# Pre-norm attention with an FP8 feed-forward on one core: the fourth key block's norm and the weight's quantisation placed ahead of the first scores

## The chip, the core and the metric

The kernel runs on one core of one Trainium2 chip. The metric is device time in microseconds for one launch. A core has TensorE (PE, with weight loads PEld beside it), VectorE (DVE), ScalarE (ACT), GpSimd (POOL) and SyncE (SP, which here only issues DMAs). Each engine works through its own instructions in order and waits on semaphores.

## The reference

```python
def reference(x, wq, bq, wk, bk, wv, bv, wo, bo, weight):   # x: (2, 2048, 512) fp32
    # attention: 16 query heads, 2 key/value heads, head size 32
    h = layernorm(x)
    q, k, v = h @ wq + bq, h @ wk + bk, h @ wv + bv
    q, k = rope(q) * 32 ** -0.5, rope(k)
    attn = softmax(q @ k.T * 32 ** -0.5)     # per head; 8 query heads share one k and v
    x = x + (attn @ v) @ wo + bo
    # feed-forward in fp8 e4m3 with one scale for the tensor
    h = layernorm(x)
    w8, w_scale = quant_e4m3(weight)         # scale = max|weight| / 448; weight: (512, 512) bf16
    h8, h_scale = quant_e4m3(h)              # scale over all 4096 rows
    return x + bf16((h8 @ w8.T) * (h_scale * w_scale))
```

The quantised weight `w8` and its scale are used by the feed-forward alone, that is, after the last row of attention is done, since `h_scale` is a maximum over all rows.

## The kernel before, in words

The 4096 rows are eight blocks of 512 (`NBLK`), four for each of two sequences. The work has three parts.

**The front** (`L697` to `L728`). The keys and values of the first sequence's four blocks are made one after another by the generator `project_kv`: `layernorm_stats` (DVE, with one power on POOL for `rstd`), `normalized` (DVE makes the tile `xn_kv`, PE transposes it, ACT copies it into `xnT`), the projection `pk` (four steps on PE, ACT adds the bias), the rotation (`r_k` on PE, `u_k` on DVE), the transposes of the values (`tv`), `rope` on POOL, and `stack_keys`: each of two arrays (`kS`, and `dkS`, the differences to a key further back) is split into a rounded and a remaining half (ACT, POOL), stored to DRAM and loaded back in four pieces, all by SP's queue. The queries of the first block come from `project_q`; `stack_queries` splits, stores and reloads them as `qst`.

The generators yield where another piece may stand between. `together` takes steps from several of them in turn, `first(steps, n)` limits one to n steps, and `run` exhausts one. The order so written is the order of the instructions on each engine. `FRONT` is 13 steps: the statistics, the normalised tiles and all transposes of a block. `MIDDLE` is 5 steps: the projection and the rotation's matmul. `PART` is 8 scores.

The front also makes the first unit's score maxima (`scores_for_maxima`): 32 score matmuls (L517) of 128 queries by 512 keys, each followed by a maximum on DVE (L524), sorted so that each eight of them need one more key block. They are taken eight at a time between the pieces of the fourth key block. The last eight need the fourth block's `kS`. Then the 8 maxima of each row are gathered, transposed and copied by ACT to `mT` (L546), and the rounds can begin.

**The rounds.** A unit is 256 queries of one quad (four heads); there are 8 units to a block and 64 in all. A unit has four rounds of four key chunks. In each round PE makes the scores again (L967) against the maxima, ACT takes the exponential (L976), POOL and an accumulating DMA add up the probabilities, and PE multiplies with the values (L913). Between these, the score maxima of the next unit are made (L517, L524), and `fill` takes pieces from a queue of jobs: the projections of later keys and queries, the output projection of finished blocks (L301, `po`) with the residual added on DVE, and the second norm. A job's step has a kind (for PE, for DVE or other) and is taken at a fixed place of the round.

`ask` puts the jobs of a block into the queue in the block's first unit, in round 2. Their inputs share a pool of three buffers (`x`), and `take_x` waits until the one three before is done. The residual's `x` of the block before is asked for only when at most two jobs are in the queue. In the last block but one, `ask` also loads the feed-forward's weight into one of these buffers and queues `prepare_weight`:

```python
            if n == NBLK - 2:
                take_x("w")
                w_all = xpool.tile([P, DC, D], BF16, tag="x", name="w_ffn")
                nc.sync.dma_start(w_all, w_ffn.rearrange("(c p) k -> p c k", p=P))
                queue.append(Job(ending(prepare_weight(w_all), "w"), due=step[0] + 2))
```

`prepare_weight` (L645 to L671) takes a maximum of each of the weight's four chunks of 128 rows on DVE (L651) and of these (L655), carries it across the partitions through two small PE instructions (L217, L223) and back to DVE for scale and inverse, and then for each chunk: scale (L663), the exponent's bits (L234), the rounding constant (L237), add (L239) and subtract (L240) on DVE, four bf16 transposes on PE (L669) and a copy by ACT into `wT` (L670). Two working tiles a chunk come from `w2`, a pool of six buffers shared with the halves of keys and queries.

**The end.** The scale over all rows is formed, and each block is quantised, transposed, multiplied with `wT` and written.

Buffers that matter here: `p` (four buffers) holds `xn_kv` in the front and the probabilities in the rounds; `ps_t` has the two PSUM banks E and O, used in the front by all transposes and in the rounds by the scores.

Of the kernel before, what the change touches and what calls it, by code (L numbers as in the profile page):

```python
# [10 lines left out]
BF16 = mybir.dt.bfloat16  # L11
# [5 lines left out]
P = 128  # L17
# [10 lines left out]
def preln_attn_fp8_ffn_kernel(  # L28
# [37 lines left out]
    nc = tc.nc  # L66
    B, S, D = x.shape
# [3 lines left out]
    DC = D // P  # L71
    NBLK = B * NB
# [15 lines left out]
    xpool = ctx.enter_context(tc.tile_pool(name="x", bufs=3))  # L88
    keys = ctx.enter_context(tc.tile_pool(name="keys", bufs=1))
    wide = ctx.enter_context(tc.tile_pool(name="wide", bufs=1))  # L90
    ppool = ctx.enter_context(tc.tile_pool(name="p", bufs=4))
# [66 lines left out]
    def load_tables(n):  # L158
        blk = n % NB
        if attending[0] or n == 0:  # L160
            csb = cs.tile([P, 2, TB], F32, tag="cs", name=f"cs_{n}")
        else:
            csb = papool.tile([P, 2, TB], F32, tag="pa", name=f"cs_{n}")
        nc.sync.dma_start(csb[:, 0, :], cos_t[:, blk * TB : (blk + 1) * TB])
        nc.sync.dma_start(csb[:, 1, :], sin_t[:, blk * TB : (blk + 1) * TB])
        return csb
# [207 lines left out]
    def project_kv(n, xt, xnT, csb):  # L374
        b, blk = divmod(n, NB)
        yield from layernorm_stats(xt, mean1[:, n, :], rstd1[:, n, :], f"1_{n}")
        yield from normalized(n, xt, xnT, f"kv_{n}")
        if n > 0:
            nc.sync.dma_start(xnT_far[n], xnT)
        if b not in vX:  # L380
            vX[b] = wide.tile([P, NTS, GROUPS, HD], F32, tag="vX", name=f"vX_{b}", bufs=2)
        pk = bank(f"pk_{n}")
        yield from product(pk, lambda c: wkv_sb[:, c, :], lambda c: xnT[:, c, :])
        if blk == 0:
            nc.gpsimd.memset(kx[:, :BACK], 0.0)
        else:
            nc.gpsimd.tensor_copy(kx[:, :BACK], kx[:, TB:])
        kv = t2(f"kv_{n}")
        nc.scalar.activation(kv, pk, AF.Identity, bias=bkv_sb)
        give_back()  # L390
        if attending[0]:
            u = swapped(kv, KD, f"k_{n}")
        else:
            u = yield from rotated(kv, csb, f"k_{n}")
        yield ON_PE
        tv = bank(f"tv_{n}")
        for i in range(NT):
            nc.tensor.transpose(tv[:, i * P : (i + 1) * P], kv[:, i * P : (i + 1) * P], ident)
        nc.scalar.copy(
            vX[b][:, blk * NT : (blk + 1) * NT, :, :].rearrange("p i g d -> p i (g d)"),  # L400
            tv.rearrange("p (i k) -> p i k", i=NT)[:, :, KD:],
        )
        give_back()
        if attending[0]:
            beside.insert(0, Job(stack_keys(n, kv, u, csb), due=step[0] + 2))
        else:
            yield from stack_keys(n, kv, u, csb)
# [238 lines left out]
    def prepare_weight(w_all):  # L646
        w = [w_all[:, o, :] for o in range(DC)]
        wmax = small.tile([P, DC], F32, tag="wmax", name="wmax")
        for o in range(DC):
            yield ON_DVE  # L650
            nc.vector.tensor_reduce(  # L651
                wmax[:, o : o + 1], w[o], AX.X, ALU.max, apply_absolute_value=True
            )
        wmax1 = small.tile([P, 1], F32, tag="wmax1", name="wmax1")
        nc.vector.tensor_reduce(wmax1, wmax, AX.X, ALU.max)  # L655
        yield LATER
        yield ON_PE
        inv = const.tile([P, 1], F32, tag="winv", name="winv")
        quantized_scale(wmax1, w_scale, inv, "w")
        for o in range(DC):  # L660
            yield ON_DVE
            v = t2(f"w_scaled_{o}")
            nc.vector.tensor_scalar(v, w[o], inv, None, ALU.mult)  # L663
            magic = t2(f"w_magic_{o}")
            yield from round_e4m3(w[o], v, magic)
            yield ON_PE
            tp = bank(f"wtp_{o}", BF16)[:, :D].rearrange("p (c t) -> p c t", c=DC)
            for c in range(DC):
                nc.tensor.transpose(tp[:, c, :], w[o][:, c * P : (c + 1) * P], ident_bf)  # L669
            nc.scalar.copy(wT[:, :, o * P : (o + 1) * P], tp)  # L670
            give_back()  # L671


    def run(steps):
        for _ in steps:
            pass
# [4 lines left out]
    def together(*runs):  # L681

        live = list(runs)
        while live:
            for steps, n in list(live):
                for _ in range(n):
                    if next(steps, "end") == "end":
                        live.remove((steps, n))
                        break

    def first(steps, n):

        for _ in range(n):
            if next(steps, "end") == "end":
                return
            yield

    FRONT = 1 + 3 * NT
# [4 lines left out]
    with tc.manual_schedule():  # L703
        xnT = {
            0: wide_block("xnT", "xnT_kv_0"),
            1: wide_block("attn", "xnT_kv_1", 2),
            2: wide_block("attn", "xnT_kv_2", 2),
            3: wide_block("qst", "xnT_kv_3", 2),
        }
        kv = {n: project_kv(n, x_kv[n], xnT[n], tables[n]) for n in (0, 1)}  # L710
        q0 = project_q(0, xnT[0], tables[0])
        run(first(kv[0], FRONT))
        together((kv[0], 1), (first(kv[1], FRONT), 2))
        x_kv[3] = load_x(3, "kv")
        kv[2] = project_kv(2, x_kv[2], xnT[2], load_tables(2))
        queries = first(q0, 1 + QUERIES)
        together((kv[1], 1), (queries, 1), (first(kv[2], FRONT), 2))
        assert (0, 0) in q_raw
        stack_queries(0)
        nc.sync.dma_start(wo_sb, wo.rearrange("(c p) n -> p c n", p=P))  # L720
        queries = first(q0, QUERIES)
        together((kv[2], 1), (queries, 1))
        kv[3] = project_kv(3, x_kv[3], xnT[3], load_tables(3))
        together((first(kv[3], FRONT), 2), (first(scores, PART), 1))
        together((first(kv[3], MIDDLE), 1), (first(scores, PART), 1))
        together((kv[3], 1), (first(scores, PART), 1))
        run(first(scores, PART))
        gather_maxima(0, ps_s.tile([P, TB], F32, tag=s_bank(), name="mtp_0"))  # L728

# [24 lines left out]
    step = [0]  # L754
# [43 lines left out]
    def take_x(name):  # L798

        while len(x_taken) >= 3 and x_taken[-3] not in x_done:  # L800
            advance()
        x_taken.append(name)

    def ending(steps, name):
        yield from steps
        x_done.add(name)
# [30 lines left out]
    def ask(u):  # L837

        k, half = units[u]

        for m in unbiased:
            add_bias(x_res[m])
            biased.add(m)
            if m in without_x:
                without_x.pop(m).due = step[0] + 2
        unbiased.clear()
        n, quad = quads[k]
        if half == 0 and quad == 0:
            if NB + n < NBLK:
                m = NB + n  # L850
                take_x(f"kv_{m}")
                make = lambda m=m: wide_block("xnT", f"xnT_kv_{m}")
                steps = later(project_kv, m, load_x(m, "kv"), make)
                queue.append(Job(ending(steps, f"kv_{m}"), due=step[0] + 2, tables=True))
            if n + 1 < NBLK:
                take_x(f"q_{n + 1}")
                steps = later(project_q, n + 1, load_xnT(n + 1))
                queue.append(Job(ending(steps, f"q_{n + 1}"), due=step[0] + 2, tables=True))
            if n == NBLK - 2:
                take_x("w")  # L860
                w_all = xpool.tile([P, DC, D], BF16, tag="x", name="w_ffn")
                nc.sync.dma_start(w_all, w_ffn.rearrange("(c p) k -> p c k", p=P))
                queue.append(Job(ending(prepare_weight(w_all), "w"), due=step[0] + 2))

        soon = len(queue) <= 2 and u % (QUADS * HALVES) > 0 or n == NBLK - 1
        free = len(x_taken) < 3 or x_taken[-3] in x_done
        if n > 0 and n - 1 not in x_asked and soon and (free or len(queue) <= 1):
            x_asked.add(n - 1)
            take_x(f"res_{n - 1}")
            x_res[n - 1] = load_x(n - 1, "res")  # L870
            unbiased.append(n - 1)
            if n == NBLK - 1:
                take_x(f"res_{n}")
                x_res[n] = load_x(n, "res")
                unbiased.append(n)
        if n == NBLK - 1 and quad == 3 and half == 0:

            fetch_y_over_keys(4, "kS", 0)
            fetch_y_over_keys(5, "dkS", 0)
# [301 lines left out]
```

## Time and profile before

| | us |
|---|---|
| median of three runs (2319.09, 2319.72, 2320.20) | 2319.72 |
| the profiled execution | 2317.02 |
| its span, from first to last instruction | 2315.2 |
| start of the first score matmul (L517) | 72.4 |
| first `mT` (end of the front) | 116.0 |
| last of the 64 `mT` | 2174.1 |

| engine | busy us | share of the span |
|---|---|---|
| PE | 2116.5 | 91% |
| POOL | 1821.6 | 79% |
| DVE | 1712.2 | 74% |
| ACT | 1237.4 | 53% |

The mean granted TensorE clock of the span is 0.967 of the full one. In the lines of the profile a row has the start, the duration, the engine, the line of the kernel, the operation and its tiles as out<-in; brackets give the engine's idle time before it and what ended it. A busy time of PE counts modelled ends, so a busy PE is not PE at its peak.

### The profile page before, as it was taken

How to read it: one execution, taken by the hardware profiler on the slowest of the kernel's cores; microseconds unless marked ns; L12 is line 12 of the kernel's file. 1: busy time of each engine (PE TensorE's matmuls, PEld its weight loads, DVE VectorE, ACT ScalarE, POOL GpSimd, SP SyncE). 2: the span in 40 equal slices, each digit the busy share in tenths (PEclk: the TensorE clock that was granted, in tenths of full speed). 3: DMA queues.
4: the chain of work that ended last, by engine and by line, in shares of the span. 5: the costliest groups of instructions: out<-in, count | busy, mean ns of one | idle time of the engine just before them, and what ended most of it. 6: DMA issues, size and time to landing. Idle time of an engine off the chain costs nothing.

```text
span 2315.2 us, 38489 instructions
## 1 busy us (share of the span) xinstructions
PE 2116.5 (91%) x15013; PEld 1229.6 (53%) x15018; DVE 1712.2 (74%) x2679; ACT 1237.4 (53%) x1545; POOL 1821.6 (79%) x1260
## 2 busy tenths in 40 slices
PE   6499999999999999999999999999999899899955
PEld 3255555555555555555555555555555555455522
DVE  3468767777778777887767778677967978767578
ACT  2146655655556555655445556555655455555646
POOL 3269888889888998889868889888988788878810
PEclk9699999999999999999999999999999899999977
DMA  6646766667586776769688667675776756868512
GB/s 199 171 102 143 158 143 158 144 152 156 124 191 147 170 158 145 166 142 208 123 205 162 122 146 162 149 136 117 154 168 132 160 119 147 168 120 211 110 53 111
DMA packets 125191, 344.70 MB, mean 149 GB/s; under 512 B 17872, under 2 KB 18512, under 8 KB 121168
## 3 DMA queue, kind: packets, MB, share of 16 engines
q0 software_dynamic: 58944, 207.64, 47.6%
q1 hardware_dynamic: 63648, 133.21, 19.5%
q8 instruction: 118, 1.93, 0.3%
q10 hardware_dynamic: 2416, 1.38, 0.2%
q14 instruction: 65, 0.53, 0.1%
HBM read 91.56 MB, written 42.99 MB: 58 GB/s over the span
## 4 chain that ended last, share of the span: by engine, by line
PE 56%; POOL 14%; DVE 12%; DMA 7%; ACT 4%; issue 4%; SPq 0%; DVEq 0%; POOLq 0%; ACTq 0%
PE s L517 17%; PE avs L913 13%; PE T L967 13%; POOL pa L950 9%; DVE part L524 6%; PE po L301 4%; DMA pa<-pa 4%; PE pq L301 4%; ACT p L976 3%; PE T L958 2%; PE avs L931 2%; POOL pa L1029 1%; DVE sw_q L319 1%; DMA qst<-q_far 1%; DVE both L889 1%
## 5 line engine op out<-in xcount | busy, mean ns | idle before, releaser
L524 DVE TENSOR_REDUCE part<-s 128x1 f32<-128x512 f32 x2048 | 1311.4, 686 | 507.2 <-PE s L517 493.4
L950 POOL TENSOR_TENSOR pa<-p,p 128x1024 f32<-128x1024 f32 x511 | 1262.0, 2528 | 218.9 <-ACT p L976 184.3
L976 ACT ACTIVATE p<-T 128x1024 f32<-128x1024 f32 x1024 | 1001.2, 1024 | 639.8 <-PE T L967 588.2
L517 PE MATMUL s<-kS,qst 128*128 128x512 f32 x2048 | 835.3, 463 | 82.1 <-DVE part L524 29.1
L967 PE MATMUL T<-qst,dkS 128*128 128x512 f32 x2048 | 687.8, 427 | 6.2 <-ACT p L976 5.0
L517 PEld LDWEIGHTS s<-kS,qst 128*128 128x128 f32 x2048 | 377.8, 191 | 458.0 <-DVE part L524 239.6
L913 PE MATMUL avs<-p,vX 128*32 128x256 f32 x8192 | 510.8, 383 | 3.3 <-ACT p L976 3.2
L967 PEld LDWEIGHTS T<-qst,dkS 128*128 128x128 f32 x2048 | 368.8, 191 | 155.7 <-issue 58.1
L913 PEld LDWEIGHTS avs<-p,vX 128*32 128x32 f32 x8192 | 231.7, 109 | 220.3 <-issue 79.3
L1029 POOL DMA_DIRECT2D pa<-pa x255 | 223.5, 877 | 80.4 <-POOL pa L950 77.0
L301 PE MATMUL po<-wo_sb,attn 128*128 128x512 f32 x256 | 130.9, 596 | 1.3 <-POOL attn L890 1.3
L889 DVE RECIPROCAL both<-both 128x128 f32<-128x128 f32 x128 | 112.5, 920 | 11.2 <-ACT both L885 11.2
L301 PE MATMUL pq<-xnT_q,wq_sb 128*128 128x512 f32 x224 | 114.4, 592 | 0.0
L931 PE MATMUL avs<-pa,ones 128*32 128x256 f32 x1024 | 79.8, 385 | 22.5 <-DMA pa<-pa 22.5
L958 PEld LDWEIGHTS T<-mT,sel 128*128 128x128 f32 x512 | 78.6, 190 | 14.2 <-ACT mT L546 3.0
L958 PE MATMUL T<-mT,sel 128*128 128x256 f32 x512 | 82.5, 283 | 1.3 <-ACT mT L546 1.3
L1031 POOL DMA_DIRECT2D pa<-pa x64 | 73.7, 1151 | 4.2 <-DMA pa<-pa 4.0
L890 POOL TENSOR_TENSOR attn<-both 128x256 f32<-128x256 f32 x64 | 66.5, 1038 | 5.9 <-DVE both L889 5.9
L546 ACT CAST mT<-mtp 128x256 fp32r<-128x256 f32 x64 | 23.9, 373 | 81.1 <-PE mtp L542 81.1
L885 ACT COPY both<-avs 128x256 f32<-128x256 f32 x63 | 23.5, 374 | 77.7 <-PE avs L931 77.7
L503 POOL TENSOR_TENSOR mrow<-mx,mrow 128x8 fp32r<-128x8 f32 x64 | 52.8, 824 | 11.7 <-ACT mrow L532 11.7
L532 ACT CAST mrow<-mx 128x8 fp32r<-128x8 f32 x64 | 13.2, 206 | 86.9 <-DVE mx L531 86.9
(127 smaller groups left out, 1206.0 us busy)
## 6 DMA issues: line engine op xcount, KB each, us to landing
pa<-pa POOLq DMA_DIRECT2D x380, 512.0 KB, 5.1
qst<-q_far SPq DMA_DIRECT2D x128, 256.0 KB, 4.8
x_kv<-in_L_attn_x_dram SPq DMA_DIRECT2D x8, 1024.0 KB, 8.6
q_far<-hi_q SPq DMA_DIRECT2D x32, 256.0 KB, 4.1
q_far<-lo_q SPq DMA_DIRECT2D x32, 256.0 KB, 3.0
x_res<-in_L_attn_x_dram SPq DMA_DIRECT2D x8, 1024.0 KB, 10.3
x_res<-in_L_attn_bo_dram POOLq DMA_DIRECT2D x8, 1024.0 KB, 12.0
out_dram<-v SPq DMA_DIRECT2D x16, 512.0 KB, 2.8
```

Of the source, the lines that this page charges most:

```text
L301: nc.tensor.matmul(dst, lhs(c), rhs(c), start=(c == 0), stop=(c == chunks - 1))
L517: nc.tensor.matmul(s, qst[k][:, j, at : at + P], stacked["kS"][:, group(k), kb * TB : (kb + 1) * TB], start=True, stop=True,)
L524: nc.vector.tensor_reduce(part[:, i, j, kb : kb + 1], s, AX.X, ALU.max)
L889: nc.vector.reciprocal(piece, piece)
L913: nc.tensor.matmul(av[j * HD : (j + 1) * HD, :], vX[batch(k)][:, kc, group(k), :], p[:, j, :], start=(kc == 0), stop=(kc == NTS - 1), tile ...
L931: nc.tensor.matmul(dst[j * HD : (j + 1) * HD, :], ones, part[:, j, :], start=start and i == 0, stop=stop and i == len(parts) - 1, tile_pos ...
L950: nc.gpsimd.tensor_tensor(pa, a, b, ALU.add)
L958: nc.tensor.matmul(T[:, j, :], sel[:, j, :], maxima[u], start=(j % 2 == 0), stop=True, skip_group_check=True,)
L967: nc.tensor.matmul(T[:, j : j + 2, :], stacked["dkS"][:, group(k), kc * P : (kc + 1) * P], qst[k][:, j : j + 2, half * HB : (half + 1) * H ...
L976: nc.scalar.activation(p, T, AF.Exp, scale=SCALE)
L1029: nc.gpsimd.dma_start(out=far_sums[r], in_=pair, accum_op=ALU.add)
L1031: nc.gpsimd.dma_start(out=far_sums[1], in_=far_sums[0], accum_op=ALU.add)
```

## The change

The weight's load stands in the front, into a buffer of the pool `p`, right behind the creation of the third block's projection. The fourth block's first 13 steps are run without scores among them, then the whole of `prepare_weight`, and then the first scores, with two steps of the fourth block's projection to a score instead of one. The 16 scores of the second and third key block go among the rest of the fourth block. The job for the weight is gone from `ask`, with its buffer of the pool `x`.

```diff
@@ -713,6 +713,8 @@
         together((kv[0], 1), (first(kv[1], FRONT), 2))
         x_kv[3] = load_x(3, "kv")
         kv[2] = project_kv(2, x_kv[2], xnT[2], load_tables(2))
+        w_all = ppool.tile([P, DC, D], BF16, tag="p", name="w_ffn")
+        nc.sync.dma_start(w_all, w_ffn.rearrange("(c p) k -> p c k", p=P))
         queries = first(q0, 1 + QUERIES)
         together((kv[1], 1), (queries, 1), (first(kv[2], FRONT), 2))
         assert (0, 0) in q_raw
@@ -721,9 +723,11 @@
         queries = first(q0, QUERIES)
         together((kv[2], 1), (queries, 1))
         kv[3] = project_kv(3, x_kv[3], xnT[3], load_tables(3))
-        together((first(kv[3], FRONT), 2), (first(scores, PART), 1))
-        together((first(kv[3], MIDDLE), 1), (first(scores, PART), 1))
-        together((kv[3], 1), (first(scores, PART), 1))
+
+        run(first(kv[3], FRONT))
+        run(prepare_weight(w_all))
+        together((first(kv[3], MIDDLE), 2), (first(scores, PART), 1))
+        together((kv[3], 1), (first(scores, 2 * PART), 1))
         run(first(scores, PART))
         gather_maxima(0, ps_s.tile([P, TB], F32, tag=s_bank(), name="mtp_0"))
 
@@ -856,11 +860,6 @@
                 take_x(f"q_{n + 1}")
                 steps = later(project_q, n + 1, load_xnT(n + 1))
                 queue.append(Job(ending(steps, f"q_{n + 1}"), due=step[0] + 2, tables=True))
-            if n == NBLK - 2:
-                take_x("w")
-                w_all = xpool.tile([P, DC, D], BF16, tag="x", name="w_ffn")
-                nc.sync.dma_start(w_all, w_ffn.rearrange("(c p) k -> p c k", p=P))
-                queue.append(Job(ending(prepare_weight(w_all), "w"), due=step[0] + 2))
 
         soon = len(queue) <= 2 and u % (QUADS * HALVES) > 0 or n == NBLK - 1
         free = len(x_taken) < 3 or x_taken[-3] in x_done
```

## The prediction

> **What bounds the kernel now.** I read the page first, then the stretches (windows) of whole query blocks, then the order of time where one block is long, and last the first 126 us, where the moved work will stand.
>
> ```profile
> PE 2116.5 (91%) x15013; PEld 1229.6 (53%) x15018; DVE 1712.2 (74%) x2679; ACT 1237.4 (53%) x1545; POOL 1821.6 (79%) x1260
> ```
>
> PE is the bound in the rounds, with DVE close behind it. So work taken out of the rounds counts if it occupies or stalls PE. A block of 512 queries runs from one block's first mT (ACT, L546) to the next one's. Blocks 5 and 6 have the same work in the rounds (a projection of queries, 32 matmuls of a query projection, 32 of an output projection, a second norm, no keys), save that block 6 also has the weight. The windows are in this order: block 5, block 6, the unit with most of the weight, and two stretches of the front:
>
> ```profile
> core 0: us, PE busy (x) PEld busy (x) DVE busy (x) ACT busy (x) POOL busy (x), PEclk, DMA share, GB/s
> 1424.60:1679.10 254.50, 247.02 (x1812) 145.30 (x1811) 194.06 (x306) 140.17 (x168) 220.57 (x149) 0.99 0.70 148
> 1679.10:1951.50 272.40, 254.96 (x1832) 150.75 (x1835) 209.52 (x319) 143.26 (x172) 220.90 (x147) 0.97 0.68 141
> 1809.60:1852.20 42.60, 33.86 (x234) 21.23 (x233) 38.52 (x52) 19.58 (x24) 30.70 (x21) 0.84 0.75 143
> 44.00:52.00 8.00, 7.32 (x23) 3.71 (x24) 0.00 (x0) 1.76 (x4) 7.15 (x6) 1.00 0.99 345
> 69.70:90.00 20.30, 11.93 (x37) 6.88 (x38) 12.43 (x24) 3.03 (x5) 1.37 (x3) 0.70 0.73 222
> ```
>
> Block 6 is 17.9 us longer. In the unit at 1809.60 DVE is busy 38.5 of 42.6 us and the clock is 0.84. The order of time shows why:
>
> ```profile
> 1811.92 2.67 DVE L237 TENSOR_SCALAR w_magic<-w_magic 128x512 f32<-128x512 f32 x1
> ...
> 1812.75 1.55 POOL L247 TENSOR_TENSOR lo_q<-q,hi_q 128x512 fp32r<-128x512 f32 x1
> ...
> 1814.52 1.87 DVE L524 TENSOR_REDUCE part<-s 128x1 f32<-128x512 f32 x3
> ...
> 1815.25 0.50 PE L517 MATMUL s<-kS,qst 128*128 128x512 f32 x1 [1.95 <-DVE part L524]
> ```
>
> A quantising instruction holds DVE, the score maxima (L524) come late, their banks stay full, and PE stands still. The waits of that unit add it up (waiter, what it waited for, us in total, times, longest):
>
> ```profile
> PE s L517 <- DVE part L524: 8.5, 4, 2.4
> ```
>
> Now the front, in order of time:
>
> ```profile
> 68.44 1.26 POOL L247 TENSOR_TENSOR lo_dkS<-dk,hi_dkS 64x512 fp32r<-64x512 f32 x1 [0.73 <-ACT hi_dkS L246]
> 72.41 1.22 PE L517 MATMUL s<-kS,qst 128*128 128x512 f32 x2 [14.60 <-DMA qst<-q_far]
> ...
> 93.50 0.68 DVE L330 TENSOR_TENSOR u_k<-r_k,cs 128x512 f32<-128x512 f32 x1
> ...
> 107.65 1.19 PE L517 MATMUL s<-kS,qst 128*128 128x512 f32 x2 [9.15 <-DMA kS<-kS_far]
> ...
> 116.00 0.37 ACT L546 CAST mT<-mtp 128x256 fp32r<-128x256 f32 x1 [1.07 <-PE mtp L542]
> ```
>
> PE stands idle before the first scores (57.8 to 72.4) and before those of the fourth key block (98.5 to 107.65). What sets 107.65 is the fourth block's chain: its rotation u_k at 93.50, POOL, the store, the reload. The change fills the first hole but moves this chain's start.
>
> **What is taken out of the rounds.** By the two windows, 272.4 - 254.5 = 17.9 us. From below: four stalls of PE, 8.5 us; clock, (1 - 0.84) x 42.6 = 6.8 us; the weight's own PE work, four groups of four bf16 transposes at 0.38 and 0.7 us for the scale, 2.2 us. Sum 17.5, so little is left unexplained. Block 6's queue then holds what block 5's holds: the residual x of block 5 is loaded at 1801.37, only after the query projection, because the weight still stood in the queue; in block 5 the like load is issued at 1436.51. The output projection and the second norm move up with it, and the second norm's last part leaves the first unit of block 7; a unit with such a norm took 27.8 us, its neighbour without it 27.0, so that is worth 0 to 0.8 us, and I take 0.5. The 0.5 MB load among the rounds is no loss or gain of its own: the x load that takes its place is larger, and block 5 has it. Removed: **18.4 us** (17 to 20; one clock stretch more or less is 1.7).
>
> A rule of the Trainium skill speaks against the clock's part: "TensorE: Matmul & The Clock Gate", in the part on the clock gate, says that the clock halves after at least one idle window of some 3.4 us. Here stalls of 1.95 to 2.38 us were each followed by 3.4 us at half clock, so the trace does not agree. Without that part the sum below would be a gain of 1.7 us; this is rival three.
>
> **What is added to the front.** (a) The weight's load now stands on SP's queue behind x and the tables of blocks 3 and 2 (42.47 to 43.46) and ahead of the second key block's stores (47.97). From 44 to 52 us the DMA engines are 0.99 busy at 345 GB/s, so 0.5 MB delays what follows by 1.5 us, and the chain from those stores runs through kv and u_q of the next stage to POOL's last piece, lo_dkS, at 68.44. The buffer that the load needs was last read before 30 us, so SP doesn't wait for it. Price 1.5 us, between 0 and rival two.
> (b) The fourth norm. Its statistics (four at 0.84) run from 60.5 as now; its rstd stands behind lo_dkS on POOL: 69.7 + 1.5 + 1.0 = 72.2. Before it was at 77.2, because DVE first waited for scores. This part starts earlier, not later.
> (c) Normalised tiles: four take 1.9 us (L267 at 14.34), but the weight holds one of the four buffers, so the fourth waits for the first's transposes, 1.1 us at half clock: 74.6. Then on DVE four maxima of the weight (two took 1.27), 2.6 us, and 0.16: 77.4. Across the partitions and back (0.27 + 0.27 + 0.38 + 0.16 + 0.16 and the handing over): 2.0 us, 79.4.
> (d) Four chunks on DVE. Undisturbed rows are 0.45, 0.43, 0.43, 0.69 and 0.69, start to start 2.75 us: 11.0 us, 90.4; the last transposes at half clock: **91.0**. Undisturbed, because POOL is busy 1.4 of the 20.3 us from 69.7 to 90. Mean rows would give 5.0 a chunk (rival one).
> (e) PE and DVE run in order, so the first scores now start at about 91.0, not 72.41, with the fourth block's projection between them. The four steps of pk take 0.86 us each at full clock and 1.7 at half; PE was sparse before, so I take half clock for 5 us, then full: with two scores 6.3 us; kv 0.7; the rotation's matmul 0.9; then the third to eighth scores at 0.65 to 0.69 for a maximum. u_k is queued behind these eight maxima: 12.4 us (10.2 all at full clock, 15.5 all at half), 103.4 instead of 93.50: 9.9 us later. Before, sixteen maxima stood ahead of u_k, now eight, which is already in this.
> (f) From u_k to the fourth block's scores 14.15 us (107.65 - 93.50), in which sixteen scores at 0.65 to 0.79, 10.3 to 12.6 us, now find room. They end sooner than the chain, so they cost nothing; beyond a chain shorter by 1.5 us they would set the end. What was the hole at 98.5 is thereby mostly filled, but the end is still the chain's.
> The weight's eight working tiles share six buffers with the third block's key halves; the last of those lands at about 83 (81.3 now), before the third chunk (84.9). On ACT only four copies of 0.59 us are added, beside DVE.
> Added: **9.9 us** (5.5 to 15).
>
> Sum: 9.9 - 18.4 = -8.5 us. The profiled execution took 2317.0 us (span 2315.2 and 1.8 around it), so its like would be 2308.5. The median of the runs shown, 2319.72, lies 2.7 above the profiled one; with the same difference the forecast is **2311.2 us**.
>
> **Rivals.** One: the quantisation costs in the front what it costs in the rounds. With the means (1.34, 0.43, 1.24, 1.33, 0.69) a chunk takes 5.0, and 4 x 2.3 = 9.2 us are added: 2320.4, no change. For it: three of four chunks were disturbed in the rounds. Against: POOL is nearly idle there.
> Two, slower: the weight's load lands ahead of the key stores as slowly as it does now.
>
> ```profile
> DMA to landing us min/median/max: 16.1/16.1/16.1
> ```
>
> Then (a) is 16.1, not 1.5: 2311.2 + 14.6 = 2325.8. It decides once the stores come 14.6 us later: 18.4 that the rounds give and 4.6 of the bound, less the other 8.4 of the cost. For it: the queue is full from 44 to 52. Against: the 16.1 us were shared with POOL's accumulating transfers, which don't run yet in the front, where 1 MB took 8.4 us.
> Three: the half-clock stretches are not the stalls' work and stay in block 6. Then 6.8 us are not regained: 2318.0, no change. Against: block 5 has one such stretch, behind a gap of 3.1 us, and none elsewhere.
>
> **How the numbers follow.** Forecast 0.70; rival one 0.13, two 0.10, three 0.07. Cheapest cost and largest gain together give 2319.7 + 5.5 - 20 = 2305, dearest and smallest 2319.7 + 15 - 17 = 2318; the range is 2304 to 2320, so that it takes in rival three and the lower half of rival one and leaves out two. 0.2%, or 4.6 us, is about what a measurement of this kernel can tell from no change. Faster by more than that (under 2315.1): 0.70 of the forecast's case less its dear end, and a little of the rivals' lower ends, 0.71. Within it 0.18, slower 0.11.
>
> **What would show it.** Right: block 6 as long as block 5 (254 us), no half clock in its third quad; DVE rows of the weight at 0.43 to 0.69; the first score near 91, u_k near 103, the first mT near 126. Wrong: a first mT at 134 or later, rows of the weight over 1 us in the front, key stores of the second block landing after 58, or a block 6 over 262 us.

## The result and the profile after

The changed kernel took 2308.7 us (median of six runs, 2301.43 to 2309.2) beside 2317.49 us for the kernel before (six runs, 2312.76 to 2320.2, the three shown above among them): a ratio of 0.9957 with a 95% interval of 0.9943 to 0.9971, which is 6.7 to 13.2 us less. The ratios here come from the measurement itself and can differ from the quotient of two medians (here 0.9962) by up to 0.001. The forecast was 2311.2 us. The profiled execution took 2304.98 us with a span of 2303.2, against 2317.02 and 2315.2 before: 12.0 us less.

The busy times on the page of the changed kernel:

```profile
PE 2117.2 (92%) x15013; PEld 1227.3 (53%) x15018; DVE 1701.2 (74%) x2679; ACT 1236.1 (54%) x1545; POOL 1819.3 (79%) x1260
```

PE has the same instructions and, within 0.7 us, the same busy time as before. That sum hides two shifts: in block 6 PE is busy 245.4 us instead of 254.9, and up to the first mT, which now holds the weight's matmuls and more half clock (0.78 granted instead of 0.84), 68.1 instead of 60.1. The stretches of the changed kernel, in the order of the prediction's table (block 5, block 6, the unit in which the weight stood, two stretches of the front):

```profile
core 0: us, PE busy (x) PEld busy (x) DVE busy (x) ACT busy (x) POOL busy (x), PEclk, DMA share, GB/s
1430.30:1685.30 255.00, 247.32 (x1812) 145.17 (x1815) 193.96 (x306) 140.10 (x168) 220.58 (x149) 0.99 0.70 147
1685.30:1937.80 252.50, 245.42 (x1812) 144.35 (x1816) 193.95 (x306) 140.04 (x169) 219.58 (x149) 1.00 0.71 148
1817.00:1850.60 33.60, 32.69 (x234) 18.87 (x233) 25.26 (x39) 17.45 (x22) 29.00 (x20) 1.00 0.69 141
44.00:52.00 8.00, 6.41 (x15) 2.47 (x13) 0.00 (x0) 1.75 (x3) 7.15 (x6) 1.00 0.99 345
69.70:90.00 20.30, 7.61 (x36) 5.46 (x37) 16.08 (x32) 4.56 (x8) 0.95 (x2) 0.50 0.73 219
```

Block 6 is now as long as block 5: 252.5 us instead of 272.4. Its third quad's first unit fell from 42.6 to 33.6 us at a clock of 1.00, and in the same unit the chain of waits shows one wait of PE for DVE where there were four with 8.5 us:

```profile
PE s L517 <- DVE x_res L573: 0.6, 1, 0.6
```

These two units don't hold the same work, though. Where the weight stood, twelve matmuls of the output projection (`po`) now stand: the job behind the weight moved up, and the last two units of block 6, which took 32.8 and 33.0 us with the output projection in them, now have none of it and take 27.4 and 27.0. So 11.4 of the 19.9 us show in the last two units, 9.1 in the weight's, 2.0 in two others, and 2.6 are lost in the unit in which the output projection now begins.

The front of the changed kernel in order of time:

```profile
41.74 0.88 SPq L717 DMA_DIRECT2D w_ffn<-in_L_ffn_weight_dram  x1
...
69.28 1.02 POOL L208 TENSOR_TENSOR rstd<-var,neg_half 128x4 f32<-128x4 f32 x1
...
80.18 0.49 DVE L663 TENSOR_SCALAR w_scaled<-w_ffn,winv 128x512 f32<-128x512 bf16 x1
80.70 0.43 DVE L234 TENSOR_SCALAR w_magic<-w_scaled 128x512 uint32<-128x512 uint32 x1
81.17 0.43 DVE L237 TENSOR_SCALAR w_magic<-w_magic 128x512 f32<-128x512 f32 x1
81.63 0.69 DVE L239 TENSOR_TENSOR w_scaled<-w_scaled,w_magic 128x512 f32<-128x512 f32 x1
82.35 0.69 DVE L240 TENSOR_TENSOR w_ffn<-w_scaled,w_magic 128x512 bf16<-128x512 f32 x1
...
92.03 1.42 PE L517 MATMUL s<-kS,qst 128*128 128x512 f32 x1
...
101.29 0.68 DVE L330 TENSOR_TENSOR u_k<-r_k,cs 128x512 f32<-128x512 f32 x1
...
114.98 1.19 PE L517 MATMUL s<-kS,qst 128*128 128x512 f32 x2 [2.50 <-DMA kS<-kS_far]
...
123.33 0.37 ACT L546 CAST mT<-mtp 128x256 fp32r<-128x256 f32 x1 [1.07 <-PE mtp L542]
```

The weight's rows run undisturbed, 2.9 us from chunk to chunk. PE waits 2.50 us for the fourth block's keys, where it waited 9.15. The first mT comes 7.3 us later than before (116.00). But 2.4 of a difference in these two executions lies ahead of everything that the change touches, in the first projection of keys. Before:

```profile
19.38 5.98 PE L301 MATMUL pk<-xnT_kv,wkv_sb 128*128 128x512 f32 x8 [0.68 <-ACT xnT_kv L292]
27.30 0.69 DVE L330 TENSOR_TENSOR u_k<-r_k,cs 128x512 f32<-128x512 f32 x1 [5.06 <-PE r_k L327]
```

After:

```profile
19.26 3.70 PE L301 MATMUL pk<-xnT_kv,wkv_sb 128*128 128x512 f32 x8 [0.67 <-ACT xnT_kv L292]
24.90 0.69 DVE L330 TENSOR_TENSOR u_k<-r_k,cs 128x512 f32<-128x512 f32 x1 [2.77 <-PE r_k L327]
```

The same eight matmuls took 2.3 us longer in the one than in the other. The granted clock reads 1.00 there in both, so the traces don't show why. In all profiled runs of this study the first u_k stands either near 25 us (24.90 to 25.83) or near 27 (26.97 to 27.62). So the front is measured below from the first u_k to the first mT ("the front's length"): 116.00 - 27.30 = 88.70 us before and 123.33 - 24.90 = 98.43 after, **+9.7**. Fronts of the same order differ by up to 1.6 us in this measure: 88.70, 89.59 and 88.00 in the kernel before, e1 and e10, and 98.43, 98.03 and 99.05 in the changed kernel, e2 and e8. The span's difference then is +9.7 (front) - 2.4 (start) - 1.1 (blocks 0 to 5) - 19.9 (block 6) + 1.7 (block 7, to the last mT) = -12.0 us, with nothing in the tail.

### The profile page after: what moved, and what is told of

It is laid out like the page before. It is cut to its first block, busy times and chain, and to the rows that moved or that the text cites. A ratio compares the mean times of both kernels' runs of the same rounds, so it can differ in the third digit from the quotient of the medians.

```text
span 2303.2 us, 38501 instructions
## 1 busy us (share of the span) xinstructions
PE 2117.2 (92%) x15013; PEld 1227.3 (53%) x15018; DVE 1701.2 (74%) x2679; ACT 1236.1 (54%) x1545; POOL 1819.3 (79%) x1260
## 4 chain that ended last, share of the span: by engine, by line
PE 57%; POOL 15%; DVE 12%; DMA 7%; ACT 4%; issue 4%; SPq 0%; DVEq 0%; ACTq 0%; POOLq 0%
PE s L517 17%; PE avs L912 13%; PE T L966 13%; POOL pa L949 10%; DVE part L524 5%; PE po L301 4%; DMA pa<-pa 4%; PE pq L301 4%; ACT p L975 3%; PE T L957 2%; PE avs L930 2%; POOL pa L1028 1%; DVE sw_q L319 1%; DMA qst<-q_far 1%; DVE v L239 1%
## 5 line engine op out<-in xcount | busy, mean ns | idle before, releaser
L524 DVE TENSOR_REDUCE part<-s 128x1 f32<-128x512 f32 x2048 | 1310.5, 685 | 499.9 <-PE s L517 485.8
L912 PEld LDWEIGHTS avs<-p,vX 128*32 128x32 f32 x8192 | 231.5, 109 | 220.2 <-issue 78.2
## 6 DMA issues: line engine op xcount, KB each, us to landing
x_res<-in_L_attn_x_dram SPq DMA_DIRECT2D x8, 1024.0 KB, 11.9
```

The costliest lines, as they stand in the source:

```text
L524: nc.vector.tensor_reduce(part[:, i, j, kb : kb + 1], s, AX.X, ALU.max)
L912: nc.tensor.matmul(av[j * HD : (j + 1) * HD, :], vX[batch(k)][:, kc, group(k), :], p[:, j, :], start=(kc == 0), stop=(kc == NTS - 1), tile ...
```

## The experiments

The first four ran on one chip (kernel before: 2315.51 us, median of 23 runs), the next four on another (2316.27, 22 runs), the last two on a third (2315.29, 17 runs). Theory T is the prediction's own: block 6 gives back 18 us because the weight no longer holds DVE there, and the front pays some 10 us because the quantisation stands ahead of the fourth block's chain.

**e1, no weight at all.** The kernel before without the weight's quantisation, which its output therefore leaves out (wT and its scale are filled with ones).

```diff
+    nc.gpsimd.memset(wT, 1.0)
+    nc.gpsimd.memset(w_scale, 1.0)
...
-            if n == NBLK - 2:
-                ...
-                queue.append(Job(ending(prepare_weight(w_all), "w"), due=step[0] + 2))
```

> The front of the kernel before and no job for the weight at all: the weight is neither loaded nor quantised (its transposed copy and its scale are filled with ones), so this shows what the rounds give back by themselves. My theory (the weight's DVE pieces hold up the score maxima, PE stands still four times and its clock halves after each stall): block 6 falls from 272.4 to about 254.5 us, the time by 18 us, ratio 0.992. The rival that the half-clock stretches have another cause and stay: block 6 near 261 us, 11 us gained, ratio 0.995, with clock 0.84 still in the third quad.

Measured: 2295.87 us, ratio 0.9924 (0.9911 to 0.9936). Front's length 89.59 us, about as before. Block 6 in the stretches of e1:

```profile
1673.30:1928.50 255.20, 247.70 (x1812) 145.96 (x1813) 194.03 (x306) 140.13 (x168) 220.13 (x149) 0.99 0.70 147
```

255.2 instead of 272.4, and no half clock in the third quad: the half-clock stretches go with the weight, and rival three falls.

**e2, the weight at both places.** The changed kernel, with the old job put back among the rounds too (its result in a second tile).

```diff
+            if n == NBLK - 2:
+                take_x("w")
+                w_again = xpool.tile([P, DC, D], BF16, tag="x", name="w_again")
+                nc.sync.dma_start(w_again, w_ffn.rearrange("(c p) k -> p c k", p=P))
+                queue.append(Job(ending(prepare_weight(w_again), "w"), due=step[0] + 2))
```

> The changed kernel with the old job for the weight left in the rounds as well (the same result is made twice): only the cost of the front against before. My theory: 9 to 10 us more than before (first mT near 124 to 126 instead of 116), ratio 1.004; block 6 as long as before, 272 us. The rival that the added work in front hides in the 14.6 us in which PE waited for the queries: ratio 1.000 to 1.001. If gain and cost add up, this ratio times that of the kernel without the weight is that of the changed kernel, 0.9957.

Measured: 2325.45 us, ratio 1.0051 (1.0037 to 1.0065), 11.8 us dearer than before by the ratio (0.0051 x 2315.5) and 9.9 by the medians: what the front pays when the rounds give nothing. The front's length is 98.03 us, as in the changed kernel, and block 6 has its cost again:

```profile
1681.60:1955.60 274.00, 251.97 (x1832) 148.90 (x1835) 212.18 (x319) 143.12 (x172) 220.85 (x147) 0.98 0.66 140
```

The two ratios multiply to 0.9924 x 1.0051 = 0.9975. That lies within the interval of e8 below, the second measurement of the change (0.9958 to 0.9985), and just above that of the first (up to 0.9971). Gain and cost add up without a third part that these times could show.

**e3, the norm alone moved.** The kernel before (its job for the weight stays), with the fourth block's first steps ahead of the scores.

```diff
-        together((first(kv[3], FRONT), 2), (first(scores, PART), 1))
-        together((first(kv[3], MIDDLE), 1), (first(scores, PART), 1))
-        together((kv[3], 1), (first(scores, PART), 1))
+        run(first(kv[3], FRONT))
+        together((first(kv[3], MIDDLE), 2), (first(scores, PART), 1))
+        together((kv[3], 1), (first(scores, 2 * PART), 1))
```

> Only the first part of the change: the fourth keys' norm and transposes run ahead of the first scores, with two projection steps to a score; the weight stays in the rounds. My theory: the norm fits into the wait for the queries (its rstd is ready at 70.7 instead of 78.2), so its transposes end near 76, u_k starts near 87 instead of 93.5 and the first mT near 110 instead of 116: 6 us faster, ratio 0.9975; all the front's cost in the changed kernel is then the weight's. The rival that the norm's place is what costs: first mT at 116 or later, ratio 1.000 or more.

Measured: 2308.54 us, ratio 0.9975 (0.9964 to 0.9987). In order of time:

```profile
86.66 0.69 DVE L330 TENSOR_TENSOR u_k<-r_k,cs 128x512 f32<-128x512 f32 x1 [1.47 <-DMA cs<-in_sin_dram]
...
99.75 1.19 PE L517 MATMUL s<-kS,qst 128*128 128x512 f32 x2 [0.89 <-DMA kS<-kS_far]
...
108.11 0.37 ACT L546 CAST mT<-mtp 128x256 fp32r<-128x256 f32 x1 [1.07 <-PE mtp L542]
```

The front's length is 81.14 us, 7.6 shorter than before. So the two halves of the edit have opposite signs in the front: the norm's move gains 7.6, and the weight behind it costs 98.43 - 81.14 = 17.3. The 9.7 is their difference. Now that u_k comes early it waits 1.47 us for its table's load, a wait that nothing in the kernel before showed. As a whole this kernel, which leaves the weight where it was, can't be told from the changed one: 0.9975 beside 0.9957 and 0.9972 (e8), with intervals that overlap. Behind the norm, the weight's move cost the front about what it gave back in the rounds (16 to 18 us, see below).

**e4, the weight alone moved.** The weight stands in the front, the fourth block's steps are run as before.

```diff
-        run(first(kv[3], FRONT))
         run(prepare_weight(w_all))
-        together((first(kv[3], MIDDLE), 2), (first(scores, PART), 1))
-        together((kv[3], 1), (first(scores, 2 * PART), 1))
+        together((first(kv[3], FRONT), 2), (first(scores, PART), 1))
+        together((first(kv[3], MIDDLE), 1), (first(scores, PART), 1))
+        together((kv[3], 1), (first(scores, PART), 1))
```

> Only the second part: the weight is quantised ahead of the first scores, right behind the second statistics of the keys before, and the fourth block's norm stays among the first scores as before. DVE is idle from 57 to 72 us, so the weight starts near 60 instead of 72.6. My theory without contention: the last transposes of the weight near 77, the first score there instead of 72.4, first mT about 5 us later than before, total 13 us faster than before, ratio 0.9944. The rival from the prediction, that DVE is held up by POOL (busy until 69.7): rows of the weight over 1 us, 5 to 9 us more, first mT 10 us or more later, ratio 0.996 to 0.998. The rows of the first two chunks tell it.

Measured: 2311.65 us, ratio 0.9983 (0.9973 to 0.9994), front's length 99.20, so 10.5 us more than before where T had expected some 5. In order of time:

```profile
68.40 1.25 POOL L247 TENSOR_TENSOR lo_dkS<-dk,hi_dkS 64x512 fp32r<-64x512 f32 x1 [0.73 <-ACT hi_dkS L246]
69.69 0.49 DVE L663 TENSOR_SCALAR w_scaled<-w_ffn,winv 128x512 f32<-128x512 bf16 x1 [4.87 <-POOL lo_dkS L247]
72.58 0.49 DVE L663 TENSOR_SCALAR w_scaled<-w_ffn,winv 128x512 f32<-128x512 bf16 x1
```

DVE stood still 4.87 us ahead of the first chunk, until POOL's last piece of the third key block was done; after it the rows were undisturbed. So the rival's 10 us came, but not by its cause: the loss against T is a wait, not slow rows. The rows don't depend on lo_dkS; the working tiles of the weight come out of the same six buffers, which e6 tries.

**e5, the load earlier.** The changed kernel with the weight's tile and load ahead of the second block's projection, so ahead of x and the tables on SP's queue.

```diff
         run(first(kv[0], FRONT))
+        w_all = ppool.tile([P, DC, D], BF16, tag="p", name="w_ffn")
+        nc.sync.dma_start(w_all, w_ffn.rearrange("(c p) k -> p c k", p=P))
         together((kv[0], 1), (first(kv[1], FRONT), 2))
...
-        w_all = ppool.tile([P, DC, D], BF16, tag="p", name="w_ffn")
-        nc.sync.dma_start(w_all, w_ffn.rearrange("(c p) k -> p c k", p=P))
```

> The changed kernel with the weight's load placed earlier on SP's queue, ahead of the second block's statistics, so that it runs near 15 to 30 us, when the DMA engines are a quarter to a third busy, and no longer stands ahead of the second block's key stores. My theory (the load delays those stores, 1.5 us predicted, 2.0 seen): from the first rotation u_k to the first mT 96.4 us instead of 98.4, the time 2 us below the changed kernel, ratio to before 0.995. The rival that the load costs nothing where it stands: 98.4 us again and 0.9957.

Measured: 2306.06 us, ratio 0.9955 (0.9939 to 0.9971), front's length 95.07 us, beside 99.05 of e8 on the same chip, 98.43 of the first profile and 98.03 of e2: 3.0 to 4.0 us less. Up to POOL's last piece of the third key block (lo_dkS, the row up to which the prediction followed the load) 1.6 to 2.1 us of it are gained: that row stands 41.02 us behind the first u_k in e5 and 42.63 to 43.16 in the other three. The rest lies behind it, in stretches that ran in part at half clock, and is not shown to be the load's. The times themselves (2306.06 and 2308.83) have ratios whose intervals overlap.

**e6, working tiles of its own.** e4, with a buffer of another pool for the weight's two working tiles.

```diff
-            v = t2(f"w_scaled_{o}")
+            work = ppool.tile([P, 2, TB], F32, tag="p", name=f"w_work_{o}")
+            v, magic = work[:, 0, :], work[:, 1, :]
             nc.vector.tensor_scalar(v, w[o], inv, None, ALU.mult)
-            magic = t2(f"w_magic_{o}")
```

> The kernel of the weight's part alone, with one edit: the weight's two working tiles of a chunk come from the pool of the normalised tiles, free at that time, and not from the six buffers shared with the halves of the keys. There the first chunk waited 4.87 us, until POOL's lo_dkS had ended, and then no row was slow. My theory: that wait was for the buffer; it goes, the first chunk starts near 65 while POOL works, some of its rows are held up to about 1 us by POOL, and the first mT comes 3 to 5 us earlier than there (94 to 96 us after the first u_k instead of 99.2), ratio to before 0.996 to 0.997. The rival that POOL's work itself held the chunk back: it starts at 69.7 again, ratio 0.998.

Measured: 2310.66 us, ratio 0.9972 (0.9959 to 0.9984), front's length 97.60 where 94 to 96 was expected. The wait is gone (the first chunk starts at 65.23, not 69.69), so it was the buffers. But the chunk that runs earlier now runs beside POOL, in order of time:

```profile
65.75 1.41 DVE L234 TENSOR_SCALAR w_work<-w_work 128x512 uint32<-128x512 uint32 x1
66.84 1.44 POOL L424 TENSOR_TENSOR dk<-kx 64x512 f32<-64x512 f32 x1
67.19 1.37 DVE L237 TENSOR_SCALAR w_work<-w_work 128x512 f32<-128x512 f32 x1
...
69.00 1.40 POOL L247 TENSOR_TENSOR lo_dkS<-dk,hi_dkS 64x512 fp32r<-64x512 f32 x1 [0.73 <-ACT hi_dkS L246]
69.32 1.63 DVE L240 TENSOR_TENSOR w_ffn<-w_work 128x512 bf16<-128x512 f32 x1
...
71.39 0.43 DVE L234 TENSOR_SCALAR w_work<-w_work 128x512 uint32<-128x512 uint32 x1
```

Of the 4.5 us won at the start the first mT keeps 1.6, no more than two fronts of the same order can differ by. L237 starts while POOL's dk runs and ends at 68.56, 0.28 after dk (68.28); L240 ends at 70.95, 0.55 after lo_dkS (70.40). Those remainders are nearly the rows' own 0.43 and 0.69: each row waited until POOL's instruction was over. The Trainium skill ("SBUF — State Buffer", section "Who interferes with whom") says that DVE and GpSimd share a pair of ports under an exclusive lock, so that the later one is blocked and not slowed. These rows agree.

**e7, the fourth block's chain first.** The weight in two parts, its maxima and scale between the fourth block's statistics and normalised tiles, its chunks beside the scores at the end; with e5's load, e6's tiles and the load of wo behind the front.

```diff
-        run(first(kv[3], FRONT))
-        run(prepare_weight(w_all))
-        together((first(kv[3], MIDDLE), 2), (first(scores, PART), 1))
-        together((kv[3], 1), (first(scores, 2 * PART), 1))
+        weight = prepare_weight(w_all)
+        run(first(kv[3], NT + 1))
+        run(first(weight, DC + 3))
+        run(first(kv[3], FRONT - NT - 1))
+        together((first(kv[3], MIDDLE), 2), (first(scores, 3), 1))
+        together((kv[3], 1), (first(scores, 3 * PART - 3), 2), (weight, 1))
```

> The changed kernel with another order in the front: the fourth block's statistics, then the weight's maxima and scale (DVE waits there for POOL's rstd anyway), then the fourth block's norm, projection and rotation with three scores among them, and only then the 21 other scores, with the rest of the fourth keys' chain and the weight's four chunks among them. The load stands early, the working tiles come from the pool of the normalised tiles, and the output weight's load stands behind the front. My theory (the cost in front is that the fourth keys' chain starts 10 us late, not the weight's 11 us on DVE): u_k near 85, the fourth block's scores wait for DVE and not for their keys, first mT 87 us after the first u_k instead of 98.4 (before: 88.7), so the front costs nothing and the rounds' 18 us remain: ratio to before 0.992. The rival that DVE's added work costs its own time wherever it stands in the front: first mT 97 or later, ratio 0.9957.

Measured: 2306.43 us, ratio 0.996 (0.9945 to 0.9976), front's length 94.49. The stretches before and behind u_k:

```profile
71.00:83.50 12.50, 9.13 (x31) 4.82 (x29) 2.48 (x5) 3.25 (x6) 0.68 (x1) 0.91 0.68 191
83.50:111.50 28.00, 15.45 (x35) 6.83 (x36) 26.33 (x42) 3.41 (x6) 6.98 (x6) 0.50 0.81 210
```

u_k came at 83.50, early enough, and the fourth keys were there at 94.5; their scores came at 111.5. DVE is busy 2.48 of the 12.5 us before u_k and 26.33 of the 28.0 behind it: with the chain out of the way the end is set by DVE's stretch behind u_k, and its idle time ahead of u_k was left unused. Neither number came: 94.49 lies between the 87 of the theory and the 97 of the rival, and as e5's early load alone gives 95.07, the new order is worth no more than 0.6. The theory falls here; e9 answers the rival's "wherever it stands".

**e8, the changed kernel again** on the chip of e5 to e7.

> The changed kernel once more beside the three others, as their base: ratio 0.9957 to before, from the first u_k to the first mT 98.4 us.

Measured: 2308.83 us, ratio 0.9972 (0.9958 to 0.9985), front's length 99.05.

**e9, two chunks in the gap.** e7, with half of the chunks ahead of u_k, where DVE idled, and all 24 scores behind it. The tables of the fourth block are loaded earlier, since u_k waited for them in e3 and e7.

```diff
+        tables[3] = load_tables(3)
         queries = first(q0, QUERIES)
         ...
-        together((first(kv[3], MIDDLE), 2), (first(scores, 3), 1))
-        together((kv[3], 1), (first(scores, 3 * PART - 3), 2), (weight, 1))
+        together((first(kv[3], MIDDLE), 2), (first(weight, 3), 1))
+        run(first(weight, 2))
+        together((kv[3], 1), (first(scores, 3 * PART), 2), (weight, 1))
```

> The order of the run with the fourth keys' chain first, with two edits: the weight's first two chunks stand before u_k, where DVE had some 10 us without work (71 to 83 us), and the 24 scores of three key blocks all stand behind u_k, with the last two chunks among them; and the fourth block's rotation tables, for which u_k waited 2.5 us there, are loaded earlier on SP's queue, right behind the first queries. Theory now: the front ends when DVE has done its work (24 maxima at 0.66, four chunks at 2.75, u_k: 28 us from 71, less the part before u_k) or when the fourth keys have landed, whichever is later. u_k near 78, the fourth block's scores near 101 (keys 92), first mT 84 us after the first u_k (before 88.7, the changed kernel 98.4 to 99.1, chain first 94.5): ratio to before 0.990 to 0.991. The rival that some other wait (banks, buffers of the key halves) takes the place: 94 us again and 0.996.

Measured: 2298.26 us (2296.35 to 2299.36), ratio 0.992 (0.9906 to 0.9934): faster than the kernel before and, the intervals not meeting those of either measurement of it, than the changed one. In order of time:

```profile
78.24 0.69 DVE L240 TENSOR_TENSOR w_ffn<-w_work 128x512 bf16<-128x512 f32 x1
81.29 0.69 DVE L330 TENSOR_TENSOR u_k<-r_k,cs 128x512 f32<-128x512 f32 x1 [2.36 <-PE r_k L327]
...
105.82 1.39 PE L517 MATMUL s<-kS,qst 128*128 128x512 f32 x2 [0.18 <-DVE part L524]
...
114.20 0.37 ACT L546 CAST mT<-mtp 128x256 fp32r<-128x256 f32 x1 [1.07 <-PE mtp L542]
```

The front's length is 87.10 us with the weight inside it, 0.9 to 2.5 shorter than in the three executions of the old front, and block 6 takes 254.3. So DVE's added work doesn't cost its own time wherever it stands. The edits against e7 (the two chunks, the scores, the tables) were not measured apart. I had expected 84: behind u_k the scores go in pairs every 1.58 us, two half-clock matmuls and their maxima, and two of the rows of the third chunk took 1.5 us instead of 0.43 and 0.48 beside POOL.

**e10, the weight spread over the rounds.** The kernel before, with the pieces of a chunk handed out one to a round (its later lines are numbered five higher).

```diff
+        yield LATER
         yield ON_DVE
         ...
+        yield LATER
+        yield ON_DVE
```

> The kernel before, with the weight left in the rounds but its DVE instructions of a chunk taken in four pieces, one to a round, instead of two pieces that may follow each other at once: the same work, shorter holds of DVE. It parts the stalls and the clock from the work itself. My theory: the four stalls of 2 us and the four half-clock stretches go or shrink (no clock under 0.95 in the third quad), about 10 of block 6's 17.9 us are regained, block 6 near 260 to 264 us, ratio to before 0.996 to 0.997. The rival that the loss is the weight's work on a full DVE, however it is cut: block 6 stays near 272 us, ratio 1.000.

Measured: 2318.38 us, ratio 1.001 (1.000 to 1.002): no gain. Block 6 itself took 264.1 us, 8.3 less and near the expected 260 to 264, though not without half clock. The unit with the weight fell from 42.7 to 36.0 us, with two half-clock stretches in it instead of four, but single pieces were still held behind POOL:

```profile
1834.59 5.22 POOL L955 TENSOR_TENSOR pa<-p,p 128x1024 f32<-128x1024 f32 x2
...
1835.83 4.53 DVE L245 TENSOR_TENSOR w_ffn<-w_scaled,w_magic 128x512 bf16<-128x512 f32 x1
```

And the job now lasted into block 7, where its end was forced through at once and PE waited for it:

```profile
1967.08 0.61 PE L674 MATMUL wtp<-ident_bf,w_ffn 128*128 128x128 bf16 x4 [5.94 <-DVE w_ffn L245]
1971.85 0.61 PE L674 MATMUL wtp<-ident_bf,w_ffn 128*128 128x128 bf16 x4 [4.16 <-DVE w_ffn L245]
```

The first unit of block 7 took 41.9 us instead of 30.8, and block 7 to its last mT 232.2 instead of 222.6, so what block 6 won was lost there. This was meant to tell the price of stalls and clock from that of the work, and doesn't: it made new stalls. How the 18 us of block 6 divide between them is open.

## Why the prediction came out right

The forecast (-8.5 us) and the change in medians (-8.8 and, by e8's pair, -7.4) agree, and the mechanism was the one predicted: block 6 lost the weight's stalls and half clock, and the fourth block's chain started later. The terms are less exact than the total. The times of the changed profile are given here with the 2.4 us of the start added, which puts them in the frame of before.

- **Taken from the rounds**, 18.4 predicted. Block 6 gave what the windows had said (17.9): it took 254.4 us on average in the eight executions without the weight in it (252.5 to 255.2) and 272.5 in the three with the old job (271.2 to 274.0), 18.1 less. Block 7, to the last mT, took 2.2 of that back: 224.0 (221.1 to 225.4) instead of 221.7 (220.4 to 222.6). That leaves 15.9, so the term was some 2.5 us too large. The 18.2 of the changed profile and the 18.7 of e1 are the largest of the eight differences to the profile of before, and the smallest is 14.8. The half clock came with the weight, for it is absent from block 6's third quad in the changed kernel and e1; that the stalls bring it is read from the rows. In the stretches of 3.4 us of the kernel before:

```profile
1812.60:1816.00 3.40, 1.46 (x7) 0.86 (x6) 3.40 (x4) 1.60 (x2) 3.40 (x3) 1.00 1.01 223
1816.00:1819.40 3.40, 3.40 (x15) 1.83 (x18) 3.03 (x6) 2.05 (x2) 0.93 (x2) 0.50 0.73 202
1819.40:1822.80 3.40, 3.40 (x46) 2.10 (x39) 3.37 (x3) 0.33 (x1) 3.10 (x3) 1.00 0.80 174
```

PE was busy 1.46 of 3.40 us, and the next stretch ran at 0.50 with 15 instead of 46 matmuls. In e10 the two half-clock stretches follow stalls of 2.42 and 1.56 us, and none follows one of 0.73. The Trainium skill's page "TensorE: Matmul & The Clock Gate", in the part on the clock gate, asks for at least one idle window of some 3.4 us; by these rows a stretch of that length that was busy 43% of the time was enough, so here the measurement decides against the page, and for the sum as the prediction made it.

- **The 0.5 us of the second norm** in that sum came out with the other sign: block 7's first unit took 32.7 to 34.8 us in those eight executions and 30.8 to 32.6 in the three. The norm did leave it (DVE busy 22.7 us instead of 24.9 in the profiles of after and before), but the unit's length doesn't follow the norm: PE waits there for POOL's accumulating transfer (`pa`), 3.3 to 4.4 us in the eight and 2.4 to 3.8 in the three. Why it waits longer is open.
- **(a) the load's delay**, 1.5, worked out up to lo_dkS: that row stood 1.5 to 2.0 us later behind the first u_k than before (42.63 to 43.16 in three executions, 41.14 before), so the term was right to half a microsecond. The second block's key stores landed 2.3 us later (29.37 us behind the first u_k instead of 27.05), at 54.3 (56.7 in the frame of before), under the 58 that would have spoken against the forecast. Rival two (16.1) was far off.
- **(b) to (d)**: rstd ended at 72.7 (72.2); the first chunk came at 79.7 (79.4); the fourth projection at 91.7 (91.0). A chunk took 2.9 us (2.75), not 5.0: rival one fell. In (b) the 72.2 is an end and the 77.2 beside it a start; the old rstd ended at 78.2.
- **(e)**: u_k 103.7 (103.4), 12.0 us behind the projection's start (12.4; the steps listed in (e) add up to 11.9). The first score itself came at 94.4, not near 91 as the list of signs had it: two steps of the projection at half clock stand ahead of it. Step (e) counts them, so the sum holds; only the sign was put on the wrong row.
- **(f)**: 13.69 us from u_k to the fourth block's scores (14.15), so that these start at 117.4 (103.4 + 14.15 = 117.6); mT 125.7 (near 126). PE still waited there, 2.50 us, so the chain set the end as said.

In the front, what (a) and (d) cost more, 0.5 and 0.4 us, was made up by (e) and (f), shorter than said by as much. That the total came so close is partly luck: the measured parts, 9.7 and 15.9, give -6.2. The interval of e8's pair (3.5 to 9.7 us less) holds this as well as the forecast, that of the first (6.7 to 13.2) only the forecast, and the blocks ahead of block 6, which no edit touches, differ by up to 8 us among the profiles (1558.5 to 1566.3). What the prediction didn't see is that its front cost was a difference of two larger terms, -7.6 for the norm and +17.3 for the weight (e3). It took the norm's move only as "earlier, not later".

The launch's start, 2.4 us in either direction, was no term of the forecast either. It is why the profiles differ by 12.0 us and by 9.6 without it.

## What to carry to other kernels

Work of DVE among rounds that PE bounds can cost more than its rows, when POOL's instructions hold it, PE stalls behind it and its clock halves: here some 13.6 us of undisturbed rows (11.0 for the chunks, 2.6 for the maxima) cost 15.9 to 18.1. Look for a stretch in which DVE and POOL are idle, and move it there. Then look at what is queued behind it in the new place: the same quantisation cost the front 17.3 us ahead of the longest chain, about what the rounds gave back, so that the norm's move alone did as well (e3). With half of it in the gap ahead of u_k and half behind, and the load and the tables earlier (e9), the front was no longer than the one before, which holds no weight, and the rounds' gain was kept. An edit with two parts is to be priced part by part, since a small sum can hide a gain worth keeping.

## What the runs showed of the hardware

- Rows of the weight's quantisation on DVE that start while POOL's two-tensor instruction runs end 0.28 or 0.55 us after it, however long that is: 0.43 became 1.37 and 1.41 (e6), 0.69 became 4.53 behind two such instructions (e10). Spreading the pieces didn't free them of it where POOL was busy 33.5 of 36.0 us. The score maxima (L524) kept their 0.6 to 0.7 us beside such an instruction (e9).
- In the front, where scores wait for their maxima, the clock stayed at 0.50 for 28 us (e7) with PE busy more than half of the time.
- The same first projection took 5.38 to 6.03 us in four of the profiled launches and 3.70 in the others, so fronts are compared from a row behind it.
